# The softplus chain of the cascade, from VectorE to ScalarE and GpSimd

## The chip, the core and the metric

The kernel runs on one core of a Trainium2 chip. The metric is the time of one execution on the device, in microseconds (us). TensorE (PE) does matrix products, VectorE (DVE), ScalarE (ACT) and GpSimd (POOL) work on tiles of 128 partitions, and SyncE's queue (SP) issues the transfers. Each engine works through its own instructions in their order and waits on semaphores for the others.

## The reference

The reference computes two layers on 8 images of 128 channels and 64x64 pixels. Layer 0 is a selective scan in four directions with a mixture of pooled experts. Layer 1 holds two kinds of state-space blocks: a small one for seeds (one pass) and a "cascade" of two blocks in a row on eight groups of channels, then a depthwise convolution and a routed mixture of experts. What this case touches is the start of each state-space block:

```python
dt = jax.nn.softplus(zxbcdt[..., -nh:] + dt_bias)
A = -jnp.exp(A_log)
y = _ssd(xs * dt[..., None], dt * A, Bm, Cm)
```

In `_ssd` the product dA = dt * A is summed along the tokens (`Acs`), and exponentials of differences of these sums are the decays that weigh each token's contribution (`Lmat`, `dec`, `cdec`). So nothing of the decays can start before dA is there.

## The kernel before

The kernel is written with a tile framework: the program names tiles and operations, and a scheduler of the framework decides at build time in what order each engine gets its instructions, within the dependencies. So a change in one helper can move other instructions of every engine as well.

`run` does layer 0 image by image, then the experts, then layer 1: `seeds` (line 1316), `cascade` (line 1336) and `second_ffn` (line 1460).

The cascade cuts the 4096 tokens of each image into segments of 256 tokens (two chunks of 128), 16 per image, 128 in all. In its loop over n one round does, for layer 0 of the cascade, the two chunks of segment n and the projection of segment n + 1, and for layer 1 the two chunks of segment n - 2 and the projection of segment n - 1. The generators `ssd_project`, `ssd_chunk` and `ssd_output` are stepped in turn, so that the work of both layers is interleaved. There are 256 projections in the cascade, two in each round, and 16 more in the seeds stage, which calls the same `ssd_project` with its own sizes.

One projection (`ssd_project`, line 943) goes like this:

- TensorE makes the projections bc_p, z_p and tok_p; ScalarE takes them from PSUM with Silu (BC, zs, tok), and DVE copies the last columns of tok_p to dtr, the raw step sizes, 128 partitions x 64 elements in the cascade and x 32 in the seeds stage (line 990). `silus_done` then loads ScalarE's table of exponentials and logarithms (line 322).
- The softplus chain (lines 1003 to 1007 and `softplus`, line 375) computes dt = ln(1 + exp(-|x|)) + max(x, 0) with a correction for the rounding of 1 + e, and dA = dt * negA. In the chain ScalarE does Abs, Exp and Ln; DVE does max (tile r), 1 + e - 1 (tile tmp), e - tmp, tmp + r, dt + tmp, and the product dA.
- `ssd_exponents` (line 915): TensorE sums dA along the tokens (the matmul cs_p), DVE splits the sums into three bfloat16 parts (csq, csr), and SP sends them through DRAM into the rows ssA and ssB, which a later chunk reads.
- Two more products of dA, dec_p and cd_p, go through Exp to wd and cd, and eA_p to eA.

One chunk (`ssd_chunk`, line 1037) makes the masked products gm, the input tiles pad, xw and xD (the last on GpSimd), the exponents ss_p from ssA and ssB, whose Exp is E_cm, the mask E_cm * gm on DVE (line 1091), the outputs y_p, and the new state S with its copy Sd on GpSimd (line 1131). `ssd_output` (line 1153) squares, averages (ms_p), scales (yz, on GpSimd) and projects (o_p).

PSUM tiles come from two rings: "a" with three places (bc_p, z_p, tok_p, ss_p, g_p and others) and "b" with two (cs_p, dec_p, cd_p, yo_s_p, y_p, o_p).

The helpers record the line of the operation: `act` is line 291, `mm` 288, `tt` 330, `ts` 334 or 336, `stt` 339. In the profile the tiles' names tell the operations apart; `_cm` stands for the cascade, `_sm` for the seeds stage.

Of the kernel before, what the change touches and what calls it, by code (L numbers as in the profile page):

```python
# [11 lines left out]
AF = mybir.ActivationFunctionType  # L12
ALU = mybir.AluOpType
# [256 lines left out]
def bc(ap, n, axis=None):  # L270

    axis = len(ap.shape) if axis is None else axis
    v = ap.unsqueeze(axis)
    shape = list(v.shape)
    shape[axis] = n
    return v.to_broadcast(shape)


class Net:
# [92 lines left out]
        self.rsqrt(sq, v, self.k(eps))  # L372
        self.tt(out, xc, sq, ALU.mult)

    def softplus(self, out, pos, neg_abs, tmp, eng):


        self.act(neg_abs, neg_abs, AF.Exp, scale=-1.0)
        self.ts(tmp, neg_abs, 1.0, ALU.add, -1.0, ALU.add)
        self.tt(tmp, neg_abs, tmp, ALU.subtract, eng)  # L380
        self.act(out, neg_abs, AF.Ln, bias=self.k("one")[: out.shape[0]])
        self.tt(tmp, tmp, pos, ALU.add, eng)
        self.tt(out, out, tmp, ALU.add, eng)


    def scan_weights(self, pool):
# [556 lines left out]
    def ssd_project(self, cfg, W, ring, stk, n_tok, wk, ps):  # L943
# [3 lines left out]
        nc = self.nc  # L947
        NP, G, nh, hd, hi, ds = cfg.np, cfg.g, cfg.nh, cfg.hd, cfg.hi, cfg.ds
        g2, NH, gh, pb, pz = cfg.g2, cfg.nhalf, cfg.gh, cfg.pb, cfg.pz
        GH = G * nh  # L950
        NC = n_tok // 128
# [9 lines left out]
        for j0 in range(0, NP, per):  # L961
            p = ps.tile([128, 2, S], F32, tag="a", bufs=self.wide, name="bc_p")
# [8 lines left out]
        p = ps.tile([128, 2, S], F32, tag="a", bufs=self.wide, name="z_p")  # L971
# [6 lines left out]
        dtr = wk.tile([128, NC, NP, g2 * nh], F32, name=f"dtr_{t_}")  # L978
        nbk, ppb = NP // cfg.ppb, cfg.ppb
        for c in range(NC):  # L980
            p = ps.tile([128, 2, S], F32, tag="a", bufs=self.wide, name="tok_p")
# [15 lines left out]
        def small(name, bufs=2):  # L997
            return wk.tile([128, NC, GH], F32, name=f"{name}_{t_}", bufs=bufs)

        dtr = dtr.rearrange("p c j f -> p c (j f)")  # L1000
        e, r, tmp, dA = (small(n) for n in ("e", "r", "tmp", "dA"))
        dt, w = (small(n, nl_) for n in ("dt", "wd"))
        self.act(e, dtr, AF.Abs)
        self.ts(r, dtr, 0.0, ALU.max)
        self.softplus(dt, r, e, tmp, nc.vector)
        self.tt(dA.rearrange("p c (g h) -> p (c g) h", h=nh), dt.rearrange("p c (g h) -> p (c g) h", h=nh),
                bc(W["negA"], NC * G, 1), ALU.mult)
        yield None
        ssA, ssB, part = self.ssd_exponents(cfg, dA, n_tok, ring, wk, ps)
        yield None  # L1010
# [1 line left out]
        p = ps.tile([128, S], F32, tag="b", bufs=self.narrow, name="dec_p")  # L1012
# [5 lines left out]
        p = ps.tile([128, S], F32, tag="b", bufs=self.narrow, name="cd_p")  # L1018
# [8 lines left out]
        p = ps.tile([128, 2, S], F32, tag="a", bufs=self.wide, name="eA_p")  # L1027
# [686 lines left out]
```

## Time and profile before

| | us |
|---|---|
| median of 3 runs | 21109.04 (21099.6 to 21120.56) |
| the profiled execution | 21100.1 |
| its span, first to last instruction | 21098.0 |
| mean granted TensorE clock | 0.928 |
| busy: TensorE, VectorE, ScalarE, GpSimd | 16896.5, 15973.0, 11555.9, 8894.3 |
| layer 0 and its experts | 0 to about 10,390 |
| seeds stage | about 10,390 to 11,370 |
| cascade | about 11,370 to 19,270 |
| second_ffn | about 19,270 to the end |

The profile was taken in one execution. PE is TensorE's matmuls, PEld its weight loads. In a list of groups a row gives line, engine, operation, tile written <- tiles read, shape, count, busy time and mean duration. In a list in order of time a row gives start, duration, engine, line and operation; the bracket at its end is how long the engine stood idle before it, and what it then had waited for. PEclk is the share of TensorE's full clock that was granted.

### The profile page before, as it was taken

The page shows a single profiled execution, that of the slowest core. Times are in us where ns is not written, and L with a number is a line of the kernel's source. Part 1 is how long each engine was busy: PE and PEld are TensorE (multiplying, and loading weights), DVE is VectorE, ACT ScalarE, POOL GpSimd, SP SyncE. Part 2 cuts the span into 40 slices and gives each one's busy share as a digit, 9 for nine tenths or more (in the row PEclk, how much of TensorE's full clock was granted, in tenths as well). Part 3 has the DMA queues.
Part 4 walks back from the last instruction along what each step waited for, and adds up shares of the span by engine and source line. Part 5 has one row for each costly group of instructions (what it writes and reads, how often), then busy time and mean ns, then how long its engine had stood idle before and what let it go on. Part 6 is the DMA issues. An engine that isn't in the chain of part 4 may idle for free. (4 is left out here: it accounts for less than half of the span.)

```text
span 21098.0 us, 301814 instructions
## 1 busy us (share of the span) xinstructions
PE 16896.5 (80%) x112733; PEld 8742.5 (41%) x112733; DVE 15973.0 (76%) x21079; ACT 11555.9 (55%) x17646; POOL 8894.3 (42%) x6004
## 2 busy tenths in 40 slices
PE   6777777777777777777887888888888888887999
PEld 2222222222222222222645666666666666664343
DVE  7979799797988979798354666666666666667886
ACT  6555555555555555555253555555555555555442
POOL 6757577575767757576011111212111121212221
PEclk9989899999999999899687999999999999998999
DMA  4434344343444434344441000000000000001110
GB/s 113 130 105 130 101 132 129 104 129 105 130 110 123 129 104 130 103 132 118 137 130 37 25 27 26 25 27 25 27 26 25 26 25 27 25 27 36 40 42 24
DMA packets 804471, 1616.93 MB, mean 77 GB/s; under 512 B 179579, under 2 KB 411931, under 8 KB 802267
## 3 DMA queue, kind: packets, MB, share of 16 engines
q1 hardware_dynamic: 803006, 1597.61, 27.6%
q8 instruction: 893, 14.63, 0.3%
q14 instruction: 572, 4.69, 0.1%
HBM read 1373.56 MB, written 223.74 MB: 76 GB/s over the span
## 5 line engine op out<-in xcount | busy, mean ns | idle before, releaser
L288 PE MATMUL dA<-parts,expand 128*128 128x512 bf16 x12288 | 3445.5, 390 | 2448.5 <-ACT dA L291 1770.3
L330 POOL TENSOR_TENSOR bx<-xE,B 128x1024 f32<-128x1024 f32 x2048 | 4823.0, 2358 | 703.7 <-DVE dA L622 461.9
L291 ACT ACTIVATE dA<-dA,negA 128x512 f32<-128x512 f32 x4096 | 2709.4, 661 | 3726.2 <-PE dA L288 3703.4
L622 DVE TENSOR_TENSOR_SCAN dA<-dA,last,bx 128x1024 f32<-128x1024 f32 x1536 | 3612.6, 2352 | 175.7 <-ACT dA L291 158.5
L288 PEld LDWEIGHTS <-expand 128*128 128x128 bf16 x12288 | 1195.4, 98 | 5231.3 <-issue 4517.6
L291 ACT ACTIVATE E_cm<-ss_p 128x1024 f32<-128x1024 f32 x2048 | 1976.9, 1030 | 1544.2 <-PE ss_p L288 1542.7
L339 DVE SCALAR_TENSOR_TENSOR E_cm<-E_cm,gm_cm 128x1024 f32<-128x1024 f32 x2048 | 2423.9, 1224 | 512.6 <-ACT E_cm L291 511.9
L330 DVE TENSOR_TENSOR hc<-dA,C 128x1024 f32<-128x1024 f32 x2048 | 2508.6, 1225 | 166.7 <-DVE dA L622 3.2
L1131 POOL COPY Sd_cm<-S_cm 64x128 f32<-64x128 f32 x1024 | 800.0, 781 | 2887.0 <-DVE S_cm L330 2754.0
L330 POOL TENSOR_TENSOR xD_cm<-tok_cm,D_cm 128x256 f32<-128x256 f32 x512 | 413.1, 807 | 2915.0 <-PE y_p L288 2795.1
L288 PE MATMUL y_p<-E_cm,pad_cm 128*32 128x128 f32 x32768 | 1389.7, 286 | 18.3 <-DVE E_cm L339 10.1
L288 PE MATMUL ss_p<-ssB_cm,ssA_cm 128*128 128x512 bf16 x4096 | 1242.6, 420 | 188.4 <-ACT E_cm L291 166.9
L622 DVE TENSOR_TENSOR_SCAN dA<-dA,bx 128x1024 f32<-128x1024 f32 x512 | 1174.1, 2293 | 185.4 <-POOL bx L330 130.2
L288 PE MATMUL y<-hc,kt 128*32 128x512 f32 x8192 | 1199.8, 653 | 26.0 <-DVE hc L330 26.0
L288 PEld LDWEIGHTS y_p<-E_cm,pad_cm 128*32 128x32 f32 x32768 | 940.5, 113 | 388.5 <-issue 240.6
L288 PE MATMUL bc_p<-stk_cm,W_cm 128*128 128x256 f32 x4096 | 1019.2, 392 | 23.8 <-DMA stk_cm<-xs 20.8
L330 DVE TENSOR_TENSOR gm_cm<-g_p,kt 128x1024 f32<-128x1024 f32 x512 | 624.3, 1219 | 505.8 <-PE g_p L288 501.0
L339 DVE SCALAR_TENSOR_TENSOR dw<-h,w_second,dw 128x512 f32<-128x512 f32 x1024 | 854.4, 860 | 5.1 <-ACT h L291 1.0
L291 ACT ACTIVATE tok_cm<-tok_p 128x384 f32<-128x384 f32 x1024 | 503.0, 491 | 605.6 <-PE tok_p L288 450.5
L288 PEld LDWEIGHTS bc_p<-stk_cm,W_cm 128*128 128x128 f32 x4096 | 739.9, 190 | 194.7 <-issue 76.8
L291 ACT ACTIVATE BC_cm<-bc_p 128x1024 f32<-128x1024 f32 x512 | 525.0, 1026 | 536.8 <-PE bc_p L288 532.4
L288 PE MATMUL tok_p<-W_cm,stk_cm 128*128 128x200 f32 x4096 | 761.4, 339 | 0.0
(387 smaller groups left out, 30190.7 us busy)
## 6 DMA issues: line engine op xcount, KB each, us to landing
xE<-dtx_d SPq DMA_DIRECT2D x2048, 512.0 KB
dtx_d<-dtx SPq DMA_DIRECT2D x256, 256.0 KB
x<-x SPq DMA_DIRECT2D x192, 256.0 KB
ssA_cm<-cs_cm SPq DMA_DIRECT2D x3072, 4.0 KB
stk_cm<-xs SPq DMA_DIRECT2D x368, 128.0 KB
stk_cm<-y SPq DMA_DIRECT2D x368, 128.0 KB
x<-in_x_dram SPq DMA_DIRECT2D x64, 256.0 KB
x<-r SPq DMA_DIRECT2D x64, 256.0 KB
```

Of the source, the lines that this page charges most:

```text
L288: self.ordered(self.nc.tensor.matmul(out, lhsT=lhsT, rhs=rhs, start=start, stop=stop))
L291: i = self.ordered(self.nc.scalar.activation(out, in_, func, **kw))
L330: self.ordered((eng or self.nc.vector).tensor_tensor(out, a, b, op))
L339: self.ordered(self.nc.vector.scalar_tensor_tensor(out=out, in0=a, scalar=s, in1=b, op0=op0, op1=op1))
L622: self.ordered(nc.vector.tensor_tensor_scan(out=t, data0=t, data1=bx.pop(n), initial=0.0 if ch["j"] == 0 else last[:, q : q + 1], op0=ALU. ...
L1131: nc.gpsimd.tensor_copy(Sd[gr, :, g * hi : (g + 1) * hi], S2[gr])
```

## The change

The softplus chain and the product dA leave DVE. ScalarE computes 1 + e with Identity and a bias of one, max(x, 0) with Relu, and Ln without a bias from 1 + e. GpSimd does the rest, five tensor-tensor operations: (1 + e) - 1, where the one is read from a constant tile of ones, e minus that, r plus that, dt plus that, and the product dA. The tiles are the same as before; r now takes part in the sum, and tmp holds 1 + e. Ln reads the tile that GpSimd then overwrites.

```diff
-    def softplus(self, out, pos, neg_abs, tmp, eng):
-        self.act(neg_abs, neg_abs, AF.Exp, scale=-1.0)
-        self.ts(tmp, neg_abs, 1.0, ALU.add, -1.0, ALU.add)
-        self.tt(tmp, neg_abs, tmp, ALU.subtract, eng)
-        self.act(out, neg_abs, AF.Ln, bias=self.k("one")[: out.shape[0]])
-        self.tt(tmp, tmp, pos, ALU.add, eng)
-        self.tt(out, out, tmp, ALU.add, eng)
+    def softplus(self, out, x, e, u, r):
+        pool = self.nc.gpsimd
+        one = self.k("one")[: out.shape[0]]
+        self.act(e, x, AF.Abs)
+        self.act(e, e, AF.Exp, scale=-1.0)
+        self.act(u, e, AF.Identity, bias=one)
+        self.act(r, x, AF.Relu)
+        self.act(out, u, AF.Ln)
+        self.tt(u, u, self.ones_.rearrange("p (c g) -> p c g", c=u.shape[1])[: out.shape[0]], ALU.subtract, pool)
+        self.tt(e, e, u, ALU.subtract, pool)
+        self.tt(r, r, e, ALU.add, pool)
+        self.tt(out, out, r, ALU.add, pool)
...
-        self.act(e, dtr, AF.Abs)
-        self.ts(r, dtr, 0.0, ALU.max)
-        self.softplus(dt, r, e, tmp, nc.vector)
+        self.ones_ = self.k("ones")[:, : NC * GH]
+        self.softplus(dt, dtr, e, tmp, r)
         self.tt(dA.rearrange("p c (g h) -> p (c g) h", h=nh), dt.rearrange("p c (g h) -> p (c g) h", h=nh),
-                bc(W["negA"], NC * G, 1), ALU.mult)
+                bc(W["negA"], NC * G, 1), ALU.mult, nc.gpsimd)
```

## The prediction

> **What bounds the kernel now.** I read the page's busy shares and slices first, then busy time by stage, then the waits of TensorE in the stage that the change touches, then two stretches of instructions in order of time. The change touches the cascade (11,370 to 19,270 us) and the seeds stage ahead of it (10,390 to 11,370); in the order in which the built programs issue instructions nothing moves in layer 0. By stage (length, then busy time and instructions of each engine, granted clock, DMA share, GB/s):
>
> ```profile
> core 0: us, PE busy (x) PEld busy (x) DVE busy (x) ACT busy (x) POOL busy (x), PEclk, DMA share, GB/s
> 10390.00:11370.00 980.00, 774.19 (x4090) 410.58 (x4090) 507.49 (x1056) 445.79 (x724) 143.59 (x232) 0.77 0.33 105
> 11370.00:19270.00 7900.00, 6980.19 (x76452) 4912.91 (x76450) 5280.05 (x10188) 4656.86 (x6770) 1530.80 (x1788) 0.94 0.09 26
> ```
>
> The cascade is TensorE's: 6980 of 7900 us busy, against 5280 on DVE. Its idle time is 920 us, and the waits (us in total, times, longest) say whose it is:
>
> ```profile
> PE cs_p L288 <- DVE dA_cm L330: 486.6, 253, 4.8
> PE ss_p L288 <- ACT E_cm L291: 166.9, 263, 2.1
> ```
>
> So over half of it is spent at the one matmul that needs dA, the last tile of the chain that is changed. A round of the cascade holds two such chains (128 rounds, 7900/128 = 61.7 us each). **Chain A** comes right behind the projection:
>
> ```profile
> 12002.78 0.46 PE L288 MATMUL y_p<-kt,xD_cm 128*128 128x128 f32 x2 [0.35 <-DVE yy_cm L330]
> ...
> 12003.78 0.26 ACT L291 ACTIVATE e_cm<-dtr_cm 128x64 f32<-128x64 f32 x1
> ...
> 12004.36 0.35 ACT L291 ACTIVATE dt_cm<-e_cm,kt 128x64 f32<-128x64 f32 x1
> ...
> 12005.43 0.22 DVE L330 TENSOR_TENSOR dA_cm<-dt_cm,negA_cm 128x64 f32<-128x64 f32 x1
> ...
> 12005.80 0.40 PE L288 MATMUL cs_p<-kt,dA_cm 128*64 128x128 f32 x2 [2.56 <-DVE dA_cm L330]
> ```
>
> TensorE stands for 2.56 us. **Chain B** runs beside GpSimd's yz:
>
> ```profile
> 11981.64 1.27 POOL L330 TENSOR_TENSOR yz_cm<-yz_cm,sq_cm 128x512 f32<-128x512 f32 x1
> 11981.76 1.22 DVE L330 TENSOR_TENSOR tmp_cm<-e_cm,tmp_cm 128x64 f32<-128x64 f32 x1
> ...
> 11983.61 0.22 DVE L330 TENSOR_TENSOR dA_cm<-dt_cm,negA_cm 128x64 f32<-128x64 f32 x1
> ...
> 11983.89 0.43 PE L288 MATMUL cs_p<-kt,dA_cm 128*64 128x128 f32 x2 [1.20 <-DVE dA_cm L330]
> ```
>
> Here TensorE stands for 1.20 us. The DVE operation that takes 0.22 us in chain A takes 1.22 beside yz: with two SBUF inputs on both engines, one waits for the other.
>
> A wait costs more than itself. Three rounds in a row, cut at chain A's cs_p (columns as above):
>
> ```profile
> 13049.91:13112.65 62.74, 55.85 (x601) 39.28 (x601) 41.50 (x80) 36.41 (x53) 11.74 (x14) 0.92 0.09 25
> 13112.65:13172.73 60.08, 53.21 (x600) 37.42 (x601) 41.48 (x80) 36.48 (x53) 12.17 (x14) 0.97 0.10 27
> 13172.73:13231.71 58.98, 51.79 (x600) 36.89 (x601) 41.57 (x81) 36.36 (x53) 12.18 (x14) 1.00 0.10 27
> ```
>
> Same work, but 58.98 us at full clock and up to 62.74 where the clock halves after the wait. The mean round (61.7) loses 2.7 us to the clock. In the rounds that I followed the drops begin around chain A's 2.56 us (now and then such a wait passes without, as at 13,172); the 1.20 us of chain B alone is not followed by one. So the limit lies between 1.2 and 2.6 us and depends on where the wait falls.
>
> **What the change does.** Per chain, six DVE operations go (r, three on tmp, dt, dA). ScalarE gets two more (Identity, Relu), five instead of three, with no added table load. GpSimd gets five TENSOR_TENSORs in series, each on the one before. There are 272 chains (256 cascade, 16 seeds). By the built order GpSimd runs Sd, Sd, then the chain, then xD at A; and xD, yz, then the chain at B. No Sd, xD or yz stands behind a chain that it needs to pass: at A xD waits for a y_p over 10 us later, at B the next Sd waits for an S some 4 us later.
>
> *One GpSimd link.* No row shows 128x64. In the seeds stage, clear of DVE, 128x512 takes 1264 ns and 128x256 takes 724, so 2.11 ns per element and 724 - 192 x 2.11 = 319 ns at 64 (estimate). Bounds: 230 (the 32x64 copy, one input) and 724. Two dependent Sd copies start 0.05 us behind each other's end; I take 0.06. Five links: 5 x 0.32 + 4 x 0.06 = 1.84 us.
>
> *Chain A.* Abs starts at 12,003.78 as before, Relu fits into the gap ahead of Exp, and dependent ScalarE operations start 0.29 apart: Ln starts 3 x 0.29 later, ends at 12,005.00. GpSimd's first link also waits for Ln (it overwrites u, which Ln reads). Handover to GpSimd 0.14 (sq to yz elsewhere), links 1.84, handover to TensorE 0.15: cs_p at 12,007.13, not 12,005.80: +1.33. But the built order now puts five ss_p matmuls ahead of cs_p; they took 1.25 to 1.6 us behind it and can start at 12,003.3. The lateness is filled, and the standing time stays about 7.13 - 4.6 = 2.5 us, merely later. What is late next: csq on DVE stands ahead of the first E_cm mask (1.22), so y_p waits about 0.8 us for it, and cd_p and yo_s_p now come late in the half; some of it returns because E_cm was evicted sooner. I take **+0.4 us**; bounds -1.3 (the five ss_p gained outright) and +1.3 (all the lateness).
>
> *Chain B.* No matmul moves ahead of cs_p. The links start when yz ends (82.91) instead of running partly beside it: dA at 84.75, cs_p at 84.81 instead of 83.89: +0.92, a wait of 2.1 us instead of 1.2. pad on DVE waits for dt and then for GpSimd's last link, and csq stands behind it; on ScalarE sq (0.65) now stands ahead of two E_cm. I take **+1.1 us**; bounds +0.6 (230 ns links) and +3.0 (724 ns).
>
> *Clock.* A's wait stays as long. B's 2.1 us is inside the open band, nearer to the 2.56 that drops. I take a drop after B in half of the rounds, at about 1.7 us (between 60.08 - 58.98 = 1.1 and 62.74 - 58.98 = 3.8): **+0.9 us**; bounds -2.7 (none left at all) and +3.8.
> [...]
>
> *Port.* [...] But by the built order DVE's next work at A stands behind csq, and at B pad behind dt, so DVE is idle while the links run, and I add nothing. If that cover is gone, one mask per chain is 256 x 1.22 = 312 us more.
>
> *Freed DVE time.* At A 1.1 us of DVE work goes, but DVE then waits for cs_p; at B it masked nothing else. Value nothing.
>
> *Seeds.* There the chain stands open too (waits up to 5.9 us at cs_p): 1.5 us x 16 = 24 us, bounds 0 and 48.
>
> *Row transfers.* The cs rows of B go out about 1.1 us later, and are now read about 2.9 us sooner. The last issue ended at 11,997.6, the new reader starts at 12,003.3; a margin of over 4 us before landing, and waits for these DMAs total under 10 us now. Nothing.
>
> **Sum.** 128 x (0.4 + 1.1 + 0.9) + 24 = 331 us on the profiled execution's own 21,100.1 us: 21,431. The median shown is 9 us above that execution, so **21,440 us**.
>
> **Rivals.**
> 1. The clock is untouched: 128 x 1.5 + 24 = 216: 21,325. For it: TensorE has other work near B. Chance 0.20.
> 2. Both waits lose the clock nearly every round, and B costs 1.5: 128 x (0.4 + 1.5 + 3.0) + 24 = 651: 21,760. For it: the two waits are both above 2 us. Chance 0.14.
> 3. Faster, by the filled wait at A: the five ss_p eat the wait until it no longer drops the clock. It decides once A's standing time falls below about 1.9 us, that is links of 0.20 rather than 0.32 us. Then the round is 58.98 + 0.6 at B = 59.6 instead of 61.7: 128 x -2.1 + 24 = -245: 20,865. Against it: only the one-input copy is that short. Chance 0.10.
> 4. Nothing to be measured: the ss_p gain at A (-1.0) pays for B: about 21,110. Chance 0.11.
> That the change doesn't take the work off DVE is excluded by the built order: the 1632 instructions are gone.
>
> **Numbers.** The forecast has 0.45, with its own range 21,330 to 21,620. 0.2% of this time (42 us) is about what a measurement can tell from no change. Faster: rival 3, 0.10. Within: rival 4, 0.11. Slower: 0.79. The range takes rivals 1 and 4 and rival 2 up to its price, and ends a little under no change: 21,080 to 21,760.
>
> **What would show it.** Right: cs_p waits on POOL, 2.2 to 2.7 us at A behind five ss_p and about 2.1 at B; links of about 320 ns; half clock also behind B; the cascade some 300 us longer, layer 0 as before. Wrong: links above 0.5 us (a port that I took for free), a clock above 0.94 in the cascade, or a DMA as the releaser of ss_p.

## The result, and the profile after

The changed kernel takes 21,352.35 us (median of 4 runs, 21,341.52 to 21,365.5); the kernel before, beside it, 21,114.8 us. The ratio is 1.0114 (95% interval 1.0099 to 1.0129): some 240 us slower. The forecast was 21,440 us. The profiled execution's span grew from 21,098.0 to 21,339.7 us.

First, where the 241.7 us lie. The stretch from the first cs_p_cm to the last, in the kernel before (the columns are those of the prediction's table by stage):

```profile
11378.75:19263.88 7885.13, 6971.37 (x76365) 4906.01 (x76365) 5272.70 (x10163) 4649.02 (x6755) 1528.78 (x1784) 0.94 0.09 26
```

and in the changed kernel:

```profile
11399.44:19509.50 8110.06, 7006.68 (x76337) 4938.42 (x76337) 4783.25 (x8633) 4699.89 (x7265) 1752.76 (x3059) 0.93 0.09 25
```

The stretch begins 20.7 us later (the seeds stage) and is 224.9 us longer (the cascade); what comes behind it is 4 us shorter. The second and third figures split the cascade's part: TensorE works 6971.4 us before and 7006.7 after, so it stands 913.8 us before and 1103.4 after. **Of the 225 us, 190 are standing time and 35 are slower work.** DVE's busy time fell by 489 us, and nothing came of it.

TensorE's waits in that stretch of the changed kernel (us in total, times, longest):

```profile
PE cs_p L288 <- POOL dA_cm L330: 662.1, 256, 6.0
...
PE ss_p L288 <- ACT E_cm L291: 130.1, 131, 1.5
PE o_p L288 <- POOL yz_cm L330: 116.0, 127, 2.9
PE y_p L288 <- DVE E_cm L339: 50.1, 71, 0.8
...
PE ss_p L288 <- DMA ssB_cm<-cs_cm: 13.5, 3, 5.8
```

The same tiles in the kernel before:

```profile
PE yo_s_p L288 <- ACT cd_cm L291: 45.4, 117, 0.4
PE o_p L288 <- POOL yz_cm L330: 45.0, 127, 3.6
...
PE ss_p L288 <- DMA ssB_cm<-cs_cm: 9.6, 3, 5.8
PE y_p L288 <- DVE E_cm L339: 8.2, 14, 0.8
```

The wait at cs_p has changed its releaser from DVE to GpSimd and grown from 486.6 to 662.1 us. At o_p TensorE waits 71 us more for yz, at y_p 42 us more for a mask; in return the wait of yo_s_p for cd_cm is gone. Waits of ss_p for a transfer stay rare. Chain A in the changed kernel, in order of time:

```profile
13058.47 1.24 PE L288 MATMUL ss_p<-ssB_cm,ssA_cm 128*128 128x512 bf16 x5
...
13060.14 0.26 ACT L291 ACTIVATE dt_cm<-tmp_cm 128x64 f32<-128x64 f32 x1
...
13060.54 0.32 POOL L330 TENSOR_TENSOR tmp_cm<-tmp_cm,kt 128x64 f32<-128x64 f32 x1 [2.02 <-ACT dt_cm L291]
...
13062.12 0.29 POOL L330 TENSOR_TENSOR dA_cm<-dt_cm,negA_cm 128x64 f32<-128x64 f32 x1
...
13062.47 0.43 PE L288 MATMUL cs_p<-kt,dA_cm 128*64 128x128 f32 x2 [2.75 <-POOL dA_cm L330]
...
13064.41 0.64 PE L288 MATMUL y_p<-E_cm,pad_cm 128*32 128x128 f32 x4 [0.75 <-DVE E_cm L339]
```

Five ss_p go first, the five links take 1.87 us from start to end, TensorE stands for 2.75 us, and y_p then waits 0.75 us for the first mask. Chain B:

```profile
13098.84 1.27 POOL L330 TENSOR_TENSOR yz_cm<-yz_cm,sq_cm 128x512 f32<-128x512 f32 x1
13100.07 0.32 POOL L330 TENSOR_TENSOR tmp_cm<-tmp_cm,kt 128x64 f32<-128x64 f32 x1
...
13101.65 0.53 POOL L330 TENSOR_TENSOR dA_cm<-dt_cm,negA_cm 128x64 f32<-128x64 f32 x1
...
13102.24 0.43 PE L288 MATMUL cs_p<-kt,dA_cm 128*64 128x128 f32 x2 [2.34 <-POOL dA_cm L330]
```

The links start when yz ends. Of the five only the last is stretched (0.53 us, against 0.29 at A): DVE's pad runs beside it. Three rounds in a row, cut at chain A's cs_p:

```profile
13062.47:13125.33 62.86, 54.00 (x601) 38.54 (x601) 37.57 (x68) 36.82 (x57) 14.91 (x24) 0.94 0.09 26
13125.33:13188.75 63.42, 55.63 (x601) 38.78 (x601) 37.76 (x68) 36.90 (x57) 12.34 (x24) 0.92 0.09 24
13188.75:13251.61 62.86, 54.00 (x600) 38.55 (x600) 37.58 (x68) 36.81 (x57) 14.91 (x24) 0.94 0.09 26
```

Rounds of 62.9 to 63.4 us, none at full clock. The trace's clock records put it in numbers: in the cascade TensorE had half clock for 932 us before (129 times, mostly 3.4 and 10.2 us in turn behind chain A) and for some 1160 us after (196 times: 6.8 us behind A in nearly each round, 3.4 us behind B in every other).

### The profile page after: what moved, and what is told of

The parts are those of the page before. It is cut to its first block, busy times and chain, and to the rows that moved or that the text cites. A ratio compares the mean times of both kernels' runs of the same rounds, so it can differ in the third digit from the quotient of the medians.

```text
span 21339.7 us, 300732 instructions
## 1 busy us (share of the span) xinstructions
PE 16955.6 (79%) x112733; PEld 8784.8 (41%) x112733; DVE 15455.4 (72%) x19447; ACT 11610.6 (54%) x18190; POOL 9137.6 (43%) x7364
## 5 line engine op out<-in xcount | busy, mean ns | idle before, releaser
L1135 POOL COPY Sd_cm<-S_cm 64x128 f32<-64x128 f32 x1024 | 603.9, 590 | 3185.2 <-DVE S_cm L330 3058.0
L288 PE MATMUL y_p<-E_cm,pad_cm 128*32 128x128 f32 x32768 | 1459.8, 295 | 58.9 <-DVE E_cm L339 52.0
L288 PE MATMUL bc_p<-stk_cm,W_cm 128*128 128x256 f32 x4096 | 1019.4, 392 | 28.5 <-DMA stk_cm<-xs 20.7
L288 PE MATMUL g_p<-BC_cm 64*128 64x128 f32 x8192 | 798.6, 325 | 0.6 <-ACT E_cm L291 0.6
```

What stands on the lines that cost most here:

```text
L288: self.ordered(self.nc.tensor.matmul(out, lhsT=lhsT, rhs=rhs, start=start, stop=stop))
L1135: nc.gpsimd.tensor_copy(Sd[gr, :, g * hi : (g + 1) * hi], S2[gr])
```

## The experiments

Twelve kernels ran, each timed beside the kernel before, whose median was 21,095 to 21,107 us. Ratios are to that. "A" and "B" are the two chains of a round. What was open: is the cost made of standing time and clock as forecast, at which chain does it arise, and what did the new place of cs_p do?

**1. The new chain at A alone.** Chain B stays on DVE with the old helper (`softplus_dve` below).

```diff
+        if W is self.ssw[0]:
             self.softplus(dt, dtr, e, tmp, r)
             ...
+        else:
+            self.act(e, dtr, AF.Abs)
+            self.ts(r, dtr, 0.0, ALU.max)
+            self.softplus_dve(dt, r, e, tmp, nc.vector)
+            ...
```

> The changed chain in chain A alone (128 of the 272); B and the seeds stage as before. Theory (TensorE stands longer at cs_p, directly and through its clock): A's five ss_p matmuls fill most of the lateness, the wait at A stays near 2.6 us, the clock falls as often as before. 0 to 0.7 us per round, 128 x 0.4 = about 50 us over the kernel before. Rival (the new order of TensorE's instructions, with cd_p and yo_s_p late, is what costs): the order changes at A, so A alone brings most of the 240 us, 150 or more.

Measured: 21,515.94 us, 1.0202 (1.0187 to 1.0217): 421 us slower, more than the whole change. The theory's number failed. The rival's number (150 or more) holds, but not its reason, since the order did not change:

```profile
15472.73 0.69 PE L288 MATMUL cs_p<-kt,dA_cm 128*64 128x128 f32 x2 [3.84 <-POOL dA_cm L330]
```

The scheduler did not put the five ss_p ahead of cs_p in this build: the wait at A is 2.56 + 1.28 us, the whole lateness. Behind it the clock was halved, mostly for 13.7 us at a time (117 times; some 1730 us of half clock in all).

**2. The new chain at B alone** (the condition turned to `self.ssw[1]`).

> The changed chain in chain B alone; A and the seeds stage as before. Theory: the wait at B goes from 1.2 to 2.3 us and half clock now follows B in about half of the rounds: 128 x 1.1 = 140 us from the wait and 20 to 80 from the clock, 160 to 220 over the kernel before. Rival (order at A): under 80 us. Rival (only both waits together lose more clock): 140 without any clock loss behind B.

Measured: 21,081.48 us, 0.9996 (0.9986 to 1.0005): no difference. The theory's number failed too; the rival's (the order at A, under 80 us) holds.

```profile
15009.93 0.40 PE L288 MATMUL cs_p<-kt,dA_cm 128*64 128x128 f32 x2 [1.49 <-DVE dA_cm L330]
15047.37 0.43 PE L288 MATMUL cs_p<-kt,dA_cm 128*64 128x128 f32 x2 [2.35 <-POOL dA_cm L330]
```

B waits 2.35 us as in the changed kernel. But at A, where the chain is still DVE's, the wait is 1.49 us and not 2.56: in this build the five ss_p are ahead of cs_p. So the order at A comes with the new chain at B: experiment 1 changed the chain alone, in the order of before, and experiment 2 changed the chain and the order. Experiments 5 and 6 take the two apart. The clock is not held here: half clock follows the 1.49 us at A in 105 of 128 rounds, and comes to some 830 us in all.

**3. The kernel before, TensorE kept at work in A's wait.** Six products of a constant tile go into cs_p's bank, which cs_p then overwrites. Work is added, none left out.

```diff
...
-        p = p[:n, :128]
+        p = full[:n, :128]
+        for _ in range(self.fill):
+            self.mm(full, self.spread[:, :128], self.spread[:, :S])
```

> The kernel before with six matmuls of constants (128x512, bfloat16, about 0.22 us each) into cs_p's own bank ahead of cs_p at chain A; cs_p overwrites them. Theory (the wait at A costs 2.7 us per round through the clock, beside itself): TensorE is seen busy in the wait, half clock goes away and a round takes near 59 us rather than 61.4: 250 to 330 us faster than the kernel before. If the clock does not matter, or falls for another reason: within 30 us, or slower by up to 128 x 0.3.

Measured: 20,804.29 us, 0.9865 (0.985 to 0.988), as the theory has it. The stretch from the first cs_p to the last:

```profile
11392.53:18986.94 7594.41, 6792.78 (x76617) 4789.53 (x77127) 5271.79 (x10163) 4637.20 (x6755) 1556.84 (x1784) 0.99 0.10 27
```

Granted clock 0.99 instead of 0.94, and 291 us less though there is more to compute. In a round of the trace VectorE, ScalarE and GpSimd have the order of before, so the fill is all that differs. What the halved clock costs the kernel before is thereby measured, and its cause is the wait at A.

**4. ScalarE's half of the change alone:** Identity and Relu on ScalarE, the five tensor-tensor operations on DVE.

```diff
-        pool = self.nc.gpsimd
+        pool = self.nc.vector
...
-                bc(W["negA"], NC * G, 1), ALU.mult, nc.gpsimd)
+                bc(W["negA"], NC * G, 1), ALU.mult)
```

> The changed formula, but the five tensor-tensor operations on DVE; only Identity and Relu move to ScalarE. Theory: a DVE link takes 0.22 to 0.28 us, so dA comes about 0.7 us later at A (partly filled) and 0.3 to 0.5 later at B than before: 40 to 130 us over the kernel before, and the rest of the 240 belongs to GpSimd's slower links. Rival (it is the two added ScalarE steps that delay the chain): over 180 us.

Measured: 21,106.32 us, 1.0005 (0.9996 to 1.0014): no difference, less than either number.

```profile
15026.27 0.49 PE L288 MATMUL g_p<-BC_cm 64*128 64x128 f32 x4
15027.47 0.43 PE L288 MATMUL cs_p<-kt,dA_cm 128*64 128x128 f32 x2 [0.70 <-DVE dA_cm L330]
...
15049.58 0.40 PE L288 MATMUL cs_p<-kt,dA_cm 128*64 128x128 f32 x2 [3.20 <-DVE dA_cm L330]
```

cs_p waits 3.20 us at A, 0.64 more: the chain on ScalarE is longer, and that is half of the 1.28 us of lateness of experiment 1. At A the order is that of before. At B cs_p waits 0.70 us, 0.50 less, but there the scheduler has put four g_p (0.49 us) ahead of cs_p, which stood behind it before. So this build, too, changed an order, and the equal time does not clear ScalarE's two steps of their share of the lateness at A.

**5. The order alone.** The kernel before, all chains on DVE, with cs_p of chain A held behind the ss_p by an order in the built program (no semaphore).

```diff
-        self.mm(p, dA.rearrange("p c g -> p (c g)"), self.k("le"))
+        i = self.mm(p, dA.rearrange("p c g -> p (c g)"), self.k("le"))
+        if self.hold:
+            self.after(i, self.ss[4])
```

> The kernel before with one thing changed: at chain A the matmul cs_p is held behind the same five ss_p as in the changed kernel; all chains stay on DVE. Theory (the order at A gains, the new chain at B costs): it has the 1.49 us wait at A that the kernel with the new chain at B alone showed, and the 1.20 us wait at B of before. Against that kernel (21,081) it saves 1.14 us of B's wait a round and a half-clock window of 3.4 us that costs about 1.2 us: 128 x 1.1 = 140 to 128 x 2.3 = 295 us, so 20,790 to 20,940. Rival (the order is worth nothing and the new chain at B costs nothing, which would also give the equal times of before and of the B-only kernel): within 40 us of before, 21,055 to 21,135.

Measured: 20,746.92 us, 0.9830 (0.9814 to 0.9847): 360 us faster, a little more than the theory's range.

```profile
15028.03 0.40 PE L289 MATMUL cs_p<-kt,dA_cm 128*64 128x128 f32 x2 [1.49 <-DVE dA_cm L331]
15064.31 0.43 PE L289 MATMUL cs_p<-kt,dA_cm 128*64 128x128 f32 x2 [1.20 <-DVE dA_cm L331]
```

```profile
11372.45:18906.04 7533.59, 6667.36 (x76365) 4739.58 (x76365) 5239.60 (x10163) 4620.45 (x6755) 1565.00 (x1784) 0.99 0.10 27
```

TensorE stands for 866 us, 48 less than before; its work, the same 76,365 matmuls, shrank by 304 us with the clock (half clock 222 us instead of 932). The clock now holds in most rounds. That is not the length of the wait alone, since experiment 2 has the same 1.49 us at A and loses the clock behind it. In this order the new chain at B then costs 1.0169 (0.9996/0.9830), 350 us, and the new chain at A on top 1.0118 (1.0114/0.9996), 250 us; in both figures the clock is included.

**6. The changed kernel without the new order:** cs_p at A held ahead of the ss_p (`self.after(self.ss[0], i)`).

> The changed kernel with one thing undone: at chain A cs_p is held ahead of the ss_p, as before; all chains stay on ScalarE and GpSimd. Theory: the order that the scheduler chose is worth 150 to 350 us to the changed kernel, and without it the kernel pays for A in full (the 421 us of the A-only kernel) and for B (140 to 295): 21,660 to 21,810. Rival (the order is worth nothing and A's and B's costs are not additive for another reason): 21,300 to 21,380, the time of the changed kernel.

Measured: 21,412.88 us, 1.0148 (1.0132 to 1.0163). Neither number was met. The order is worth 0.3% (some 70 us) to the changed kernel, not 1.7% as to the kernel before, and the kernel is 0.5% faster than A alone, though chain B is late here as well. The order is not quite that of before: the 24 yo_s_p of this half, which stood ahead of most of its y_p, now come behind them.

```profile
11416.14:19578.81 8162.67, 6930.82 (x76336) 4883.85 (x76337) 4844.85 (x8633) 4714.08 (x7265) 1919.09 (x3059) 0.94 0.09 25
```

Standing time is 1231.9 us, 318 more than before: the lateness of both chains is 128 x (1.28 + 1.14) = 310. Here the standing time adds up. The clock does not: half clock was some 990 us here, against some 1730 with A alone. The halved stretches lie on a grid of 3.41 us (see the last section). That the place of the waits on this grid, and not the moved yo_s_p, makes the difference is likely but not shown.

**7. The changed kernel filled at both waits**, 8 constant products at A behind the fifth ss_p, 3 products of e at B.

> The changed kernel with its order kept, and with TensorE kept busy in both waits: at A 8 products of a constant 128x512 tile into cs_p's bank between the fifth ss_p and cs_p, at B 3 products of the tile e, which GpSimd's second link writes; cs_p then overwrites them. Work is added, none left out. Theory: the clock stays above 0.97 in the cascade, so that what is left over the filled kernel before (20,804) is the waits alone, predicted as 0.4 + 1.1 us a round and 24 us in the seeds: 20,950 to 21,030. Rival 1 (all of the change's cost is clock): 20,800 to 20,850. Rival 2 (all of it is waits): 21,040 or more.

Measured: 21,199.01 us, 1.0042 (1.0027 to 1.0057), above the theory's range and rival 1's. It lies in that of rival 2 (21,040 or more), but not for rival 2's reason. The trace shows another: DVE's order had changed with the build, and the first mask ran beside the links.

```profile
15335.86 0.32 POOL L332 TENSOR_TENSOR e_cm<-e_cm,tmp_cm 128x64 f32<-128x64 f32 x1
15336.26 1.40 POOL L332 TENSOR_TENSOR r_cm<-r_cm,e_cm 128x64 f32<-128x64 f32 x1
15336.27 1.23 DVE L341 SCALAR_TENSOR_TENSOR E_cm<-E_cm,gm_cm 128x1024 f32<-128x1024 f32 x1 [2.34 <-ACT E_cm L293]
```

One link takes 1.40 instead of 0.32 us and cs_p comes 1.1 us later. So it does not decide between waits and clock, but it measures the cover that the prediction's port step relied on.

**8. The same, with DVE's order around chain A held as in the changed kernel.**

> The filled changed kernel again, with VectorE's order around chain A held as in the changed kernel (csq ahead of the first E_cm mask; in the fill before, the mask had come ahead and one GpSimd link beside it took 1.40 us instead of 0.32). 8 constant products at A, 3 products of e at B. Theory: links of 0.32 us again, clock above 0.97, round of 60.0 to 60.3 us at full clock against 58.90 in the filled kernel before, which is 128 x 1.2 + 21 us in the seeds = 175 us over 20,804: 20,940 to 21,040. Rival (the clock is the whole cost): 20,800 to 20,850.

Measured: 20,961.3 us, 0.9932 (0.9917 to 0.9947), in the theory's range.

```profile
11409.86:19125.28 7715.42, 6942.09 (x78149) 4918.70 (x78149) 4738.41 (x8633) 4717.41 (x7265) 2005.42 (x3059) 0.99 0.09 26
```

The links are 0.32 us again and the clock is 0.99. Against the filled kernel before it stands at 1.0068 (0.9932/0.9865), 141 us: with the clock held in both, the change still costs its standing time. One order differs from the changed kernel (some g_p stand ahead of y_p and fill the 0.75 us wait there), so the 141 us are a lower value for it. In the cascade it is 7715.4 less 7594.4, 121 us or 0.95 us a round.

**9. The kernel before, with the order of 5 and four constant products.**

> The kernel before with cs_p at A held behind five ss_p, and 4 products of a constant 128x512 tile into cs_p's bank between them. Theory: 1.1 us of A's wait is filled with work that has to be done anyway, on top of the clock: 128 x 1.1 = 140 us below the filled kernel before (20,804): 20,640 to 20,700. Rival (what is gained at A is given back behind it, at the masks and the late dec_p and cd_p): 20,780 to 20,830.

Measured: 20,648.37 us, 0.9783 (0.9768 to 0.9798): 459 us faster than before, the fastest of all, and as the theory has it. It beats both kernels.

**10. The changed kernel with B's links ahead of yz on GpSimd.**

```diff
+            if self.yz_ is not None:
+                self.after(self.yz_, i)
```

(i is the operation that writes dA at B, yz_ that of layer 0's yz.)

> The changed kernel with one order changed on GpSimd: at chain B the five links go ahead of layer 0's yz, not behind it. Theory (B's lateness is the place in GpSimd's queue, behind yz's 1.27 us): cs_p at B waits 0.9 to 1.0 us instead of 2.34, the half clock behind B goes, and 128 x (1.4 + about 0.6 of clock) = 255 us are saved: 21,000 to 21,170. Rival (the links' own length makes B late, or the later yz is waited for at o_p): 21,300 to 21,380.

Measured: 21,150.46 us, 1.0023 (1.0014 to 1.0032): 190 us faster than the changed kernel, at the high end of the theory's range.

```profile
15001.70 0.69 PE L289 MATMUL cs_p<-kt,dA_cm 128*64 128x128 f32 x2 [2.75 <-POOL dA_cm L331]
15039.69 0.43 PE L289 MATMUL cs_p<-kt,dA_cm 128*64 128x128 f32 x2 [1.12 <-POOL dA_cm L331]
```

B waits 1.12 us, less than DVE's chain needed (1.20), with the same five links. In a round of the trace the order of TensorE, VectorE and ScalarE is that of the changed kernel, and half clock behind B is gone from all but a few rounds. So B's lateness is the place behind yz, not the links.

**11. The same for the kernel with the new chain at B alone.**

> The new chain at B alone, ahead of yz on GpSimd; chain A on VectorE as before, in the order of that kernel (cs_p at A behind five ss_p, wait 1.49 us). Theory: waits of 1.49 at A and 0.9 to 1.0 at B, both under the point from which the clock drops, so a full-clock round of about 57.9 us: 20,660 to 20,760, faster than before by 350 us or more. Rival (the later yz is waited for at o_p, or A's 1.49 us still drops the clock): 20,900 to 21,100.

Measured: 20,794.01 us, 0.9854 (0.9838 to 0.9871): 309 us faster than before, 34 us over the theory's range. Waits are 1.49 us at A and 1.11 at B, half clock 256 us. Against the order alone (0.9830) nothing is gained by GpSimd; it is 0.2% behind.

**12. The new chain at A alone, in its order, filled** with 11 constant products ahead of cs_p.

> The kernel with the new chain at A alone, its order kept (cs_p ahead of the ss_p), and 11 constant 128x512 products into cs_p's bank ahead of cs_p at A. Theory (A's 3.84 us wait costs its 1.28 us of lateness, and all the rest of that kernel's 421 us was half clock, 1727 us of it): without the half clock it stands 164 to 200 us, the lateness or the standing time that it added, above the filled kernel before (20,804): 20,960 to 21,020, some 500 us below the same kernel unfilled (21,516). Rival (the 421 us come from work behind the late cs_p, not from the clock): 21,200 or more.

Measured: 20,951.24 us, 0.9926 (0.9909 to 0.9942), just under the theory's range.

```profile
11422.35:19136.62 7714.27, 6999.10 (x77762) 4870.53 (x77762) 5131.40 (x9400) 4681.27 (x7009) 1875.81 (x2419) 0.99 0.09 26
```

Half clock falls from some 1730 to some 140 us, and the time by 565 us. What is left over the filled kernel before is 0.62% (0.9926/0.9865), 129 us, where the lateness alone is 128 x 1.28 = 164. So 1.28 us of lateness at A cost 421 us because some 290 of them were clock (421 less 129).

In the kernels of 1 to 4 some 500 to 630 of TensorE's 76,000 matmul records are missing; their standing time is therefore not given.

## Why the prediction was right

The forecast was right in its sign and in its mechanism: cs_p stands longer at both chains, and half clock now follows B too. The clock's term was too large, and some of what fits does so by luck. The time, 21,352 us, lies 88 us under the forecast and only 27 above rival 1 (the clock untouched), but what rival 1 supposes did not happen: TensorE had some 1160 us of half clock instead of 932.

- **One GpSimd link, 0.32 us, gap 0.06.** The median of each of the first four links is 317 to 318 ns, dA takes 0.29 (A) and 0.53 us (B, beside pad); starts are 0.39 to 0.40 apart. Right.
- **Chain A, +0.4 us a round, wait about 2.5, y_p then 0.8.** The waits are 2.75 and 0.75 us. In the sum: the standing time grew by 190 us, 1.48 a round; chain B's is 1.14 (2.34 less 1.20), which leaves 0.34 for A, the new order included. This is a remainder, and right in part by luck: cs_p at A waits 0.19 us more and y_p 0.33 more, as forecast, but the forecast had cd_p and yo_s_p come late, while the wait of yo_s_p for cd_cm went away (0.35 less), and it did not see that o_p would wait 0.55 us more for yz. That wait does not need the new links: in experiment 5, with the new order and DVE's chains, it is 123.6 us. What the step did not see either is what the order is worth by itself: with DVE's chain it takes A's wait to 1.49 us and 360 us off the kernel (experiment 5). The scheduler gave that, and the longer chain took it back.
- **Chain B, +1.1 us, wait 2.1.** Measured 1.14, wait 2.34; the reason (the links stand behind yz) is shown by experiment 10. Right, though in part by luck: the working gave cs_p 0.92 us of lateness and added 0.2 for work behind it, and the 0.2 came ahead of cs_p instead, in the one link that pad stretches.
- **Clock, +0.9 us: A's as before, a drop behind B in half of the rounds.** The event was right: A has 6.8 us of half clock in nearly each round (before 3.4 and 10.2 in turn, the same mean), B has 3.4 us in every other. Its price was the mis-sized term, taken at 1.7 us for a drop. Of the three rounds shown after, the one with a drop behind B is 63.42 us long and its neighbours 62.86, 0.56 us apart (its work is 1.63 us longer, but TensorE stands 1.07 us less in it). Where experiment 10 takes the drops behind B away, the stretch of the cascade falls by 207 us, of which 128 x (2.34 - 1.12) = 156 are B's wait; the rest, 51 us, is 0.8 us for each of some 65 drops. By these two readings a drop cost 0.6 to 0.8 us. The 1.7 lay between two rows of which the lower (60.08 less 58.98, 1.1 us) belonged to a drop of that length; the upper was one of 10.2 us. The lower one would have been nearer.
- **Port, nothing.** Held at A, by DVE's order alone. At B it did not quite hold: pad needs dt, but not the last link, dA, which therefore runs beside pad and takes 0.24 us longer than at A. Where a mask ran beside the links (experiment 7) one link took 1.40 us, 1.08 more, near the 1.22 that the prediction gave as the price of the lost cover.
- **Freed DVE time, nothing.** 489 us of DVE time gone, the cascade longer. **Seeds, 24 us.** Measured 20.7. **Row transfers, nothing.** 13.5 us of waits instead of 9.6.
- **Sum.** Forecast 128 x (0.4 + 1.1 + 0.9) + 24 = 331 us. By the trace's busy time the result is 128 x (0.34 + 1.14 + 0.28) + 20.7 = 246, less 4 us behind the cascade; 0.28 is the 35 us of slower work in 128 rounds. How it splits is less sure than that it adds up, since slower work can also cover standing time (in the rows above 1.63 us more work goes with 1.07 us less standing). The two filled kernels (experiments 8 and 3), with the clock held in both, put 0.95 us a round on standing time, a lower value, where the trace puts 1.48; then up to 0.8 us is clock. By either, the standing time is the larger part, and the clock's 0.9 was too much. The time lies in the range.
- **Rival 3** (faster, once A's wait falls below about 1.9 us) did not come about here, but its mechanism is real: experiments 5 and 9 are that case, with a wait of 1.49 us and, filled, of 0.53.

Of the expectations on the way those of experiments 1, 2, 4, 6 and 7 missed; 1 and 2 (A alone at about no cost, B alone at a clear one) since I took the order of the changed kernel for that of its halves. What stays open: why the scheduler moves cs_p at A when chain B gets longer, and a rule by which the number of repeated half-clock stretches could be told ahead.

## What to carry to other kernels

Count a dependent chain by two things: the standing time that it leaves on the bound engine, which added up here from chain to chain (experiment 6: 318 us, of which the two chains' lateness is 310), and the clock that the standing time costs behind it, which did not (some 990 us of half clock with both chains late, some 1730 with A alone), so price that by a row whose stretch has the same length. Ahead of a matmul that must wait, place work that is due anyway (here five ss_p, 360 us) or even constant products (290 us): each is more than the 240 us that the change of engines cost. Half of a change may be scheduled otherwise than the whole, so compare the issue order of each build before you add up their times. And two builds of equal time need not have equal waits: experiment 2 takes 21,081 us with waits of 1.49 (A) and 2.35 us (B), experiment 4 21,106 us with 3.20 and 0.70. A clock that falls in every round may hide the difference (last section).

## What the hardware showed that was not expected

- The clock fell behind the sum of several waits (1.49 and 0.75 us in most rounds of experiment 2). In the traces of the kernel before and of the changed one all onsets of half clock, 350 and 423 in the whole execution, lie within 0.01 us of one grid of 3.413 us: no wait shifted it. In the cascade the half clock lasts 3.4, 6.8, 10.2 or 13.7 us, multiples of it (in a few cases more of them). In the changed kernel each of the 3.41 us stretches ahead of an onset holds at least 1.60 us of standing time in all (median 2.23); of the stretches that no onset follows none holds more than 1.90 and some ten hold more than 1.5. In the kernel of experiment 5 some onsets follow 1.3 to 1.6 us, so no sharp limit shows. The waits of 1.49 us (cs_p) and 0.75 us (y_p) behind A are the same in experiments 5 and 2. In most rounds of experiment 2 they fall into one stretch and the clock drops; in most of experiment 5 they do not, and it holds.
- A round whose clock falls every time seems to settle on the grid. From chain A's cs_p to the next one, over a hundred rounds in the middle, the mean round is 61.45 us before, 61.44 in experiments 4 and 10 and 61.23 in experiment 2, which is 18.00, 18.00, 18.00 and 17.94 stretches of 3.413 us; in the changed kernel it is 63.13 us, 18.50 stretches (37.0 for two rounds, as in the rows shown), and in experiment 1 64.65 us, 18.94. Where half clock is rare the round has no such length (17.18 in experiment 5, 17.32 in 3), and experiments 6 and 7, at 18.60 and 18.14, lie between. So experiments 2 and 4 may equal the kernel before because they settle on the same 18 stretches, and half a stretch a round, 1.7 us or 218 us in the cascade, is nearly all that the change costs there (224.9). This is read from the lengths alone; no run moved a wait in small steps to test it.
- A GpSimd link beside one mask of DVE took 1.40 us instead of 0.32 (experiment 7), 1.08 more, which is most of the mask's 1.23 us, and ended 0.16 us behind the mask. In the kernel before, GpSimd's Sd takes 1.23 us where it meets a mask (median of 259) and 0.29 alone, and DVE's e - tmp 1.22 us beside yz (124 times) and 0.23 alone. Two inputs on both engines, as the prediction has it, are not needed: Sd has one, and so has DVE's 1 + e - 1, which takes 0.72 us beside xD (124 times) and 0.20 alone.
- Products of a constant tile, whose results nothing uses, took 1.35% off the kernel before (experiment 3), and with the order 2.17% (experiment 9).
